# A four-layer graph network on one core: roots on GpSimd, an adjacency scaled once, and another way of ordering the instructions

## The chip, the core and the metric

The kernel runs on one core of a Trainium2 chip. A core has TensorE for matrix products, VectorE and ScalarE for elementwise work, GpSimd (POOL in the profile) and SyncE, whose queue (SP) issues every DMA here. Each engine works through its own list of instructions in order; semaphores tie the lists together. The metric is the device time of one execution in microseconds; the times before are 5736.96, 5727.94 and 5721.77 us, with a median of 5727.94.

## What is computed

Sixty-four graphs of 256 nodes with 128 features, and a symmetric 0/1 adjacency of about 12% ones with a full diagonal, go through four layers. Each layer adds its result to its input and normalizes (`_layernorm`). Cut to what matters:

```python
def layer0(x, adj):      # edge network with a maximum over neighbours
    pre = (x @ (W1 - W2))[:, :, None, :] + (x @ W2)[:, None, :, :] + b
    return max(relu(pre) * adj[..., None], axis=2)

def layer1(x, adj):      # three branches, two of them aggregated
    upd = concat([adj @ elu(x @ W_in.T + b_in), elu(x @ W_node.T + b_node),
                  adj.T @ elu(x @ W_out.T + b_out)])
    return tanh(upd @ W_upd.T + b_upd)

def layer2(x, adj):      # graph convolution with a normalized adjacency
    A = adj + eye;  deg = A.sum(-1)
    dinv = where(deg > 0, rsqrt(deg), 0)
    nA = dinv[:, None] * A * dinv[None, :]
    h = elu(elu(x @ W0 + b0))
    h = elu(nA @ (h @ W1) + b1)
    return nA @ (h @ W2) + b2

def layer3(x, adj):      # a message for every edge, normalized, through gelu
    pre = (x @ W1a)[:, None, :, :] + (x @ W1b)[:, :, None, :] + b1
    msg = gelu(layernorm(pre) * g1 + be1)
    agg = einsum('bijo,bij->bio', msg, adj)
    return layernorm(concat([x, agg]) @ W2 + b2) * g2 + be2
```

## The kernel before

It uses the sparsity. `first` sorts the nodes of a graph by degree (L551 to L560: signs, their sum, a permutation `perm`), ranks every neighbour and writes one-hot columns `hot` (L629): one column of 4800 for every kept slot of every half of the nodes. A product with `hot` then gathers neighbours' values, so layers 0 and 3 work on 2 x 4800 columns and not on 256 x 256 edges.

A graph passes through four stages, each a Python generator: `first` (layer 0: the sort, `hot`, the gathers L665 and the folds of the maximum at L492), `second` (layer 1), `third` (layer 2, the values for layer 3, and the first four tiles of it), `last` (the other tiles and the output). Layer 3's 9600 columns are cut into ten tiles a graph, in each half four of 1024 and one of 704 (`TODO`). For a tile, `sums_of` gathers with L728, adds `dT` at L732 (VectorE), squares (L736, ScalarE), sums over features on TensorE (L743), and makes the variance row at L745 (ScalarE). The row goes to memory (`line<-row`, L750). Two tiles make a pair: the pair's variances come back spread over partitions (`vr<-line`, L762), get a root and a reciprocal (`inverse_root`), are multiplied by the mask `fu` (L769), go out again (`scale_line<-vr`, L771), and each tile's scales return broadcast to all partitions (`rs_s<-scale_line`, L828). In `last`, L839 multiplies a tile by its scales, L841 applies Gelu, and the folds at L492 and the products at L860 gather the messages.

`together` runs the four stages of four successive graphs side by side and so records the instructions of all 64 graphs in one program without a loop. That recorded order isn't the one that runs: when the kernel is built, a scheduler with a model of the engines reorders the instructions of each engine and hands out tile buffers. The order on an engine is then fixed. An ACT_TABLE_LOAD stands before an activation whose function isn't in the table set then loaded; Gelu, the exponential with the hyperbolic tangent, and the root are in three sets.

`inverse_root` is used for layernorms (five a graph, L176), for the degrees (L272) and for pairs of tiles (L768):

```python
def inverse_root(t):
    nc.scalar.activation(t, t, AF.Sqrt)
    nc.vector.reciprocal(t, t)
```

In layer 2 the rows of `hs` are scaled by `dinv` ahead of each of the two products with the adjacency (L293), and the result is scaled once more at L309. The degrees `dg` are summed in `first` (L544); the rest of their work stands in layer 2, two stages later. The adjacency `aT` is used by layer 1 (L238) before layer 2 adds the identity to it (L277).

A second path, `general`, stands behind a test at the end, for inputs that the sparse path doesn't cover; with these inputs it doesn't run. The change touches it where it shares functions.

Of the kernel before, what the change touches and what calls it, by code (L numbers as in the profile page):

```python
# [9 lines left out]
F32 = mybir.dt.float32  # L10
BF16 = mybir.dt.bfloat16
AF = mybir.ActivationFunctionType
ALU = mybir.AluOpType
# [6 lines left out]
P = 128  # L20
EPS = 1e-5
# [22 lines left out]
def kernel(  # L44
# [9 lines left out]
    nc = tc.nc  # L54
    B, N, D = x.shape
    assert N == 2 * P and D == P
    H = N // P
    Q = P // 4

    consts = ctx.enter_context(tc.tile_pool(name="consts", bufs=1))  # L60
# [6 lines left out]
    eps_t = consts.tile([P, 1], F32, name="eps_t")  # L67
    nc.vector.memset(eps_t, EPS)
    minus1 = consts.tile([P, 1], F32, name="minus1")
    nc.vector.memset(minus1, -1.0)  # L70

    def inverse_root(t):

        nc.scalar.activation(t, t, AF.Sqrt)  # L74
        nc.vector.reciprocal(t, t)

    def load(src, shape, name):
        t = consts.tile(shape, F32, name=name)
# [43 lines left out]
    with tc.tile_pool(name="prep", bufs=1) as prep, tc.tile_pool(  # L122
        name="ps_prep", bufs=2, space=bass.MemoryType.PSUM
# [33 lines left out]
    class Shared:  # L157
# [8 lines left out]
        def layernorm(self, dst, src, g=None, be=None):  # L166

            st = self.work.tile([P, H, 6], F32, name="st", bufs=4)
            mv = self.work.tile([P, H, 2], F32, name="mv", bufs=4)
            for h in range(H):  # L170
                nc.vector.bn_stats(st[:, h], src[:, h])
                nc.vector.bn_aggr(mv[:, h], st[:, h])
            rs = self.work.tile([P, H], F32, name="rs", bufs=4)
            nc.vector.tensor_scalar(rs, mv[:, :, 1], EPS, None, ALU.add)
            yield
            inverse_root(rs)  # L176
            yield
            for h in range(H):
                if g is None:
                    nc.vector.tensor_scalar(  # L180
                        dst[:, h], src[:, h], mv[:, h, 0:1], rs[:, h:h + 1], ALU.subtract, ALU.mult
                    )
                else:
                    nc.vector.scalar_tensor_tensor(dst[:, h], src[:, h], mv[:, h, 0:1], g, ALU.subtract, ALU.mult)
                    nc.vector.scalar_tensor_tensor(dst[:, h], dst[:, h], rs[:, h:h + 1], be, ALU.mult, ALU.add)
# [17 lines left out]
        def to_features(self, xn, name, bufs=None):  # L203

            pt = self.psum()
            for h in range(H):
                nc.tensor.transpose(pt[:, h * P:(h + 1) * P], xn[:, h], ident)
            t = self.state.tile([P, N], F32, name=name, **({"bufs": bufs} if bufs else {}))
            nc.scalar.copy(t, pt[:, :N])
            return t  # L210

        def node_tile(self, name):
            return self.state.tile([P, H, P], F32, name=name)
# [44 lines left out]
            yield from self.layernorm(x2, y)  # L258
            s["x2"] = x2

        def layer_2(self, s, aT, deg_of):

            work, psum, elu = self.work, self.psum, self.elu
            x2 = s["x2"]
            deg = work.tile([P, H], F32, name="deg")
            deg_of(deg)
            nc.vector.tensor_scalar(deg, deg, 1.0, None, ALU.add)
            pos = work.tile([P, H], F32, name="pos")
            nc.vector.tensor_scalar(pos, deg, 0.0, None, ALU.is_gt)
            dinv = work.tile([P, H], F32, name="dinv")  # L270
            nc.vector.tensor_scalar(dinv, deg, 1e-30, None, ALU.max)
            inverse_root(dinv)  # L272
            yield
            nc.vector.tensor_mul(dinv, dinv, pos)
            for h in range(H):
                blk = aT[:, h, h * P:(h + 1) * P]
                nc.vector.tensor_add(blk, blk, ident)  # L277
            yield
            xT = self.to_features(x2, "xT_2", 1)
            yield  # L280
            ph = psum()
            hs = work.tile([P, H, P], F32, name="hs")
            for h in range(H):
                cols = slice(h * P, (h + 1) * P)
                nc.tensor.matmul(ph[:, cols], xT[:, cols], w2[0], start=True, stop=True)
            yield
            for h in range(H):
                nc.vector.tensor_add(hs[:, h], ph[:, h * P:(h + 1) * P], b2[0])
            yield from elu(hs, hs, twice=True)
            yield  # L290
            for step in (1, 2):
                for h in range(H):
                    nc.vector.tensor_scalar(hs[:, h], hs[:, h], dinv[:, h:h + 1], None, ALU.mult)  # L293
                pa = psum()
                for h in range(H):
                    nc.tensor.matmul(pa[:, :N], hs[:, h], aT[:, h], start=h == 0, stop=h == H - 1)  # L296
                yield
                agg = work.tile([P, N], F32, name="agg")
                nc.scalar.copy(agg, pa[:, :N])
                yield  # L300
                po = psum()
                for h in range(H):
                    cols = slice(h * P, (h + 1) * P)
                    nc.tensor.matmul(po[:, cols], agg[:, cols], w2[step], start=True, stop=True)
                yield
                hs = work.tile([P, H, P], F32, name="hs")
                for h in range(H):
                    nc.vector.scalar_tensor_tensor(
                        hs[:, h], po[:, h * P:(h + 1) * P], dinv[:, h:h + 1], b2[step], ALU.mult, ALU.add  # L309
                    )  # L310
                if step == 1:
                    yield from elu(hs, hs)
                yield
            nc.vector.tensor_add(hs, hs, x2)
            x3 = self.node_tile("x3")
            yield from self.layernorm(x3, hs)
            s["x3"] = x3
# [36 lines left out]
    def sparse(ctx):  # L354
# [35 lines left out]
        with tc.tile_pool(name="cs_prep", bufs=1) as pp:  # L390
            t = pp.tile([P, P], F32, name="upto_f")
# [4 lines left out]
            t = pp.tile([P, N], I32, name="iota_i")  # L396
# [28 lines left out]
            t = pp.tile([P, 1], F32, name="gbe")  # L425
# [76 lines left out]
        def first(g, s):  # L502
# [37 lines left out]
            nc.scalar.activation(diff, diff, AF.Abs, accum_out=fl[:, 0:1])  # L540
            kc = work.tile([P, H, H], F32, name="kc")
            nc.vector.scalar_tensor_tensor(kc, pc, -1.0, down_c, ALU.mult, ALU.subtract)
            dg = state.tile([P, H], F32, name="dg", bufs=3)
            nc.vector.tensor_reduce(dg, pc, AX.X, ALU.add)  # L544
            s["dg"] = dg

            more = work.tile([P, H, H], F32, name="more")
            for h in range(H):
# [169 lines left out]
        def sums_of(s, i):  # L718
# [47 lines left out]
                s["fulls"].rearrange("h w -> (h w)")[first_at:first_at + n].rearrange("(p k) -> p k", k=PIECE),  # L766
            )
            inverse_root(vr[:rows])  # L768
            nc.vector.tensor_mul(vr[:rows], vr[:rows], fu[:rows])  # L769
            out_line = dram.tile([1, GROUP * TILE], F32, name="scale_line")  # L770
            nc.sync.dma_start(out_line[:, :n].rearrange("o (p k) -> (o p) k", k=PIECE), vr[:rows])  # L771
            at = 0
# [8 lines left out]

        def third(g, s):

            dg = s["dg"]

            def deg_of(deg):
                nc.vector.tensor_scalar(deg, dg, 1.0 / N, None, ALU.mult)

            yield from sh.layer_2(s, s["aT"], deg_of)
            yield  # L790
            x3, perm = s["x3"], s["perm"]

            x3T = sh.to_features(x3, "x3T")
            yield
            pc = psum()
            for h in range(H):
                nc.tensor.matmul(
                    pc[:, h * N:(h + 1) * N], x3T[:, h * P:(h + 1) * P], w3c.rearrange("p c o -> p (c o)"),
                    start=True, stop=True,
                )  # L800
            pcv = pc.rearrange("p (h c o) -> p h c o", h=H, c=2)
            dn = work.tile([P, H, P], F32, name="dn")
            nc.scalar.copy(dn, pcv[:, :, 1])
            c3 = state.tile([P, 3, H, P], BF16, name="c3")
            split3(c3, pcv[:, :, 0])
            yield
            pd = psum()
            for h in range(H):
                for hi in range(H):
                    nc.tensor.matmul(  # L810
                        pd[:, h * N:(h + 1) * N], dn[:, hi], perm[:, h, hi], start=hi == 0, stop=hi == H - 1
                    )
            yield
            dT = state.tile([P, H, N], F32, name="dT")
            nc.scalar.activation(dT, pd.rearrange("p (h n) -> p h n", h=H), AF.Identity, bias=b3c)
            s.update(x3T=x3T, c3=c3, dT=dT)
            yield
            for i in range(AHEAD):
                yield from sums_of(s, i)
# [61 lines left out]
        def steps(g0):  # L881
            ss = [{} for _ in range(U)]
            for u in range(1 - len(STAGES), U):
                together(*[
                    (n, part(g0 + u + i, ss[u + i])) for i, (part, n) in enumerate(STAGES) if 0 <= u + i < U
                ])

        if U == B:
            steps(0)
        else:  # L890
            with tc.For_i(0, B, U) as g0:
                steps(g0)


    def general(ctx):
# [82 lines left out]
        def middle(g, s):  # L978
# [7 lines left out]
                nc.scalar.copy(aT[:, hj], pt[:, :N])  # L986
            yield

            def deg_of(deg):
                nc.vector.tensor_reduce(deg, an, AX.X, ALU.add)  # L990

            yield from sh.layer_1(s, an, aT, s["x1"])
            yield
            yield from sh.layer_2(s, aT, deg_of)
            yield

            x3T = sh.to_features(s["x3"], "x3T")
# [145 lines left out]
```

## Time and profile before

| | |
|---|---|
| median of the three runs | 5727.94 us |
| the profiled execution | 5731.62 us, span 5729.7 us |
| granted TensorE clock, mean | 0.862 |
| DMA | 20% of 16 engines' time, 64 GB/s on average |
| Gelu, L841, 640 tiles | 594.2 us for the 512 into `pre`, 1172 ns each |
| first gathers, L665 | 1052.3 us in 3840 matmuls |
| gathers for layer 3, L728 | 928.8 us in 3840 matmuls |
| adds of dT, L732 | 846.3 us in 1664 instructions |
| scaling by rs_s, L839 | 732.9 us in 640 instructions |
| one-hot columns, L629 | 440.5 us in 1536 instructions |

The profile is of one execution. Its rows of busy time give for each engine the time in which some instruction of it ran; matmuls are pipelined, so a busy TensorE isn't TensorE at its peak. A row of a group reads: line, engine, operation, tile written and tile read, shape, count, then busy time and mean nanoseconds of one, then the time that the engine stood idle ahead of it and what ended the wait. "Waits" list who waited for whom, with the total, the number of times and the longest. The chain is the work that ended last, followed back from the last instruction.

### The profile page before, as it was taken

How to read it: one execution, taken by the hardware profiler on the slowest of the kernel's cores; microseconds unless marked ns; L12 is line 12 of the kernel's file. 1: busy time of each engine (PE TensorE's matmuls, PEld its weight loads, DVE VectorE, ACT ScalarE, POOL GpSimd, SP SyncE). 2: the span in 40 equal slices, each digit the busy share in tenths (PEclk: the TensorE clock that was granted, in tenths of full speed). 3: DMA queues.
4: the chain of work that ended last, by engine and by line, in shares of the span. 5: the costliest groups of instructions: out<-in, count | busy, mean ns of one | idle time of the engine just before them, and what ended most of it. 6: DMA issues, size and time to landing. Idle time of an engine off the chain costs nothing.

```text
span 5729.7 us, 83531 instructions
## 1 busy us (share of the span) xinstructions
PE 4529.9 (79%) x27408; PEld 2508.7 (44%) x27408; DVE 4834.4 (84%) x14654; ACT 4275.2 (75%) x6485; POOL 1.9 (0%) x10
## 2 busy tenths in 40 slices
PE   5878878878778778788788788787887887877875
PEld 2444444444444444444444444444444444444443
DVE  6788888888888888888888888888888888888876
ACT  2577777777777777777777777777777777777785
POOL 0000000000000000000000000000000000000000
PEclk8888889889889889888898898898888887888986
DMA  0122222222212221221221222122212212221222
GB/s 22 44 70 63 62 63 72 62 63 66 69 57 70 65 63 63 72 63 62 63 72 62 63 65 70 59 68 65 63 62 72 64 62 63 69 66 60 68 65 74
DMA packets 292813, 365.15 MB, mean 64 GB/s; under 512 B 151952, under 2 KB 210448, under 8 KB 292368
## 3 DMA queue, kind: packets, MB, share of 16 engines
q1 hardware_dynamic: 292368, 359.73, 20.0%
q8 instruction: 217, 3.56, 0.3%
q14 instruction: 228, 1.87, 0.1%
HBM read 345.07 MB, written 14.53 MB: 63 GB/s over the span
## 4 chain that ended last, share of the span: by engine, by line
PE 52%; DVE 29%; ACT 11%; issue 4%; DMA 3%; SPq 0%; DVEq 0%; POOL 0%; ACTq 0%
PE bigp L665 11%; PE bigp L728 8%; DVE pre L839 6%; PE mm L860 5%; DVE lanes L492 4%; PE mm L743 4%; DVE hot L629 4%; DVE pre L732 4%; DVE sums L492 3%; PE bigp L681 3%; DMA rs_s<-scale_line 2%; PE mm L870 2%; PE mm L296 2%; PE mm L699 2%; PE mm L647 2%
## 5 line engine op out<-in xcount | busy, mean ns | idle before, releaser
L665 PE MATMUL bigp<-hot,q 128*128 128x512 fp8e4 (+1 forms) x3840 | 1052.3, 371 | 66.6 <-DVE lanes L492 52.6
L728 PE MATMUL bigp<-hot,c 128*128 128x512 fp8e4 (+1 forms) x3840 | 928.8, 372 | 140.2 <-DVE pre L732 140.2
L732 DVE TENSOR_TENSOR pre<-bigp,dT 128x512 f32<-128x512 f32 (+6 forms) x1664 | 846.3, 530 | 37.8 <-PE bigp L728 33.5
L492 DVE TENSOR_TENSOR lanes<-bigp,lanes 128x512 f32<-128x512 f32 (+6 forms) x1536 | 772.7, 503 | 94.6 <-PE bigp L681 86.9
L839 DVE TENSOR_TENSOR pre<-pre,rs_s 128x1024 f32<-128x1024 f32 (+1 forms) x640 | 732.9, 1150 | 48.6 <-DMA rs_s<-scale_line 48.0
L736 ACT ACTIVATE sq<-pre 128x1024 f32<-128x1024 f32 (+1 forms) x640 | 638.5, 998 | 169.9 <-DVE pre L732 163.9
L841 ACT ACT_TABLE_LOAD x535 | 686.4, 1283 | 9.5
L492 DVE TENSOR_TENSOR sums<-pre,sums 128x1024 f32<-128x1024 f32 (+6 forms) x1024 | 628.8, 614 | 41.2 <-ACT pre L841 40.7
L745 ACT ACTIVATE row<-mm,eps_t 128x256 f32<-128x256 f32 (+1 forms) x640 | 289.6, 453 | 476.9 <-PE mm L743 476.7
L841 ACT ACTIVATE pre<-pre,be,g 128x1024 f32<-128x1024 f32 (+1 forms) x512 | 594.2, 1172 | 57.8 <-DVE pre L839 53.0
L743 PE MATMUL mm<-sq,ones 128*32 128x256 f32 (+1 forms) x5120 | 482.9, 440 | 135.2 <-ACT sq L736 135.2
L74 ACT ACT_TABLE_LOAD x445 | 570.9, 1283 | 7.5
L728 PEld LDWEIGHTS <-c 128*128 128x128 bf16 x3840 | 331.2, 98 | 550.5 <-issue 136.1
L665 PEld LDWEIGHTS <-q 128*128 128x128 bf16 x3840 | 310.8, 97 | 392.6 <-issue 112.0
L296 PE MATMUL mm<-aT,hs 128*128 128x256 f32 x512 | 232.3, 600 | 316.1 <-DVE hs L293 214.8
L629 DVE TENSOR_SCALAR hot<-rank 128x512 fp8e4<-128x512 bf16 (+5 forms) x1536 | 440.5, 348 | 0.0
L681 PEld LDWEIGHTS <-pick 42*128 42x128 bf16 x2944 | 155.8, 95 | 481.5 <-issue 474.2
L296 PEld LDWEIGHTS mm<-aT,hs 128*128 128x128 f32 x512 | 135.6, 293 | 425.8 <-issue 316.1
L860 PE MATMUL mm<-w3u,sums 128*128 128x128 f32 x2048 | 296.7, 289 | 18.4 <-DVE sums L492 16.1
L194 ACT ACT_TABLE_LOAD x221 | 283.5, 1283 | 3.9
L681 PE MATMUL bigp<-lack,pick 42*128 42x36 bf16 (+16 forms) x2944 | 285.7, 187 | 0.0
L860 PEld LDWEIGHTS mm<-w3u,sums 128*128 128x128 f32 x2048 | 254.5, 195 | 37.3 <-issue 17.6
(226 smaller groups left out, 7132.6 us busy)
## 6 DMA issues: line engine op xcount, KB each, us to landing
rs_s<-scale_line SPq DMA_DIRECT2D x512, 512.0 KB
rs_s<-scale_line SPq DMA_DIRECT2D x128, 352.0 KB
an<-in_adj SPq DMA_DIRECT2D x64, 256.0 KB
x<-in_x SPq DMA_DIRECT2D x64, 128.0 KB
line<-row SPq DMA_DIRECT2D x512, 4.0 KB
out<-o SPq DMA_DIRECT2D x64, 128.0 KB
fu<-fulls SPq DMA_DIRECT2D x192, 4.0 KB
vr<-line SPq DMA_DIRECT2D x192, 8.0 KB
```

The lines of the kernel that those rows point to most:

```text
L74: nc.scalar.activation(t, t, AF.Sqrt)
L492: nc.vector.tensor_tensor(lanes[:, :k, :w], src[:, i:i + k], lanes[:, :k, :w], op)
L629: nc.vector.tensor_scalar(hot[:, :, at:at + w], rank[:, :, :w], s0 + i + 1.0 - FAR, None, ALU.is_equal, saturate=False)
L665: nc.tensor.matmul(pt[:, :tl], q3[:, i, h], hot[:, h, t0:t0 + tl], start=i == 0, stop=False)
L681: nc.tensor.matmul(o_, l_, r_, start=False, stop=i == len(todo) - 1)
L728: nc.tensor.matmul(pt[:, :bl], c3[:, k, h], hot[:, h, t0 + b:t0 + b + bl], start=k == 0, stop=k == 2)
L732: nc.vector.tensor_add(block(pre[:, b:], n, w, at), block(pt, n, w, at), widen(dT[:, h, :w], n))
L736: nc.scalar.activation(sq[:, :tl], pre[:, :tl], AF.Square)
L743: nc.tensor.matmul(pr[q * Q:(q + 1) * Q, :tl // 4], ones[:, :Q], v4[:, :, q], start=True, stop=True)
L839: nc.vector.tensor_mul(pre[:, :tl], pre[:, :tl], rs[:, :tl])
L841: nc.scalar.activation(msg[:, :tl], pre[:, :tl], AF.Gelu, bias=be3, scale=g3)
L860: nc.tensor.matmul(pt[:, cols], lanes[:, k, cols], w3u[:, 1], start=k == 0, stop=False)
```

## The change

Five edits:

- `inverse_root` becomes one power of -0.5 on GpSimd, against a constant tile. It now serves the pairs and the degrees alone. The multiplication of a pair's scales by the mask goes to GpSimd as well.
- A layernorm takes its root on ScalarE with the small constant as the activation's bias, which drops an addition on VectorE; the reciprocal stays there. Where the generator yields also changes.
- The degrees' inverse root moves from layer 2 to `first`, into `inverse_root_of`, and its product with the mask goes to GpSimd. The result lives in four buffers until layer 2 takes it.
- In layer 2, `dinv` is multiplied into the rows of the adjacency once, in two instructions of 128x256, in place of scaling `hs` ahead of both products in four of 128x128.
- The unrolled body stands in a block of its own, for which the scheduler orders instructions with a finer model of the engines.

```diff
+    mhalf = consts.tile([P, 16], F32, name="mhalf")
+    nc.vector.memset(mhalf, -0.5)
+
     def inverse_root(t):
 
-        nc.scalar.activation(t, t, AF.Sqrt)
-        nc.vector.reciprocal(t, t)
+        nc.gpsimd.tensor_tensor(t, t, mhalf[:t.shape[0], :t.free_size()], ALU.pow)
...
                 nc.vector.bn_stats(st[:, h], src[:, h])
                 nc.vector.bn_aggr(mv[:, h], st[:, h])
+            yield
             rs = self.work.tile([P, H], F32, name="rs", bufs=4)
-            nc.vector.tensor_scalar(rs, mv[:, :, 1], EPS, None, ALU.add)
-            yield
-            inverse_root(rs)
-            yield
+            nc.scalar.activation(rs, mv[:, :, 1], AF.Sqrt, bias=eps_t)
+            yield
+            nc.vector.reciprocal(rs, rs)
...
+        def inverse_root_of(self, deg, bufs):
+
+            nc.vector.tensor_scalar(deg, deg, 1.0, None, ALU.add)
+            pos = self.work.tile([P, H], F32, name="pos")
+            nc.vector.tensor_scalar(pos, deg, 0.0, None, ALU.is_gt)
+            dinv = self.state.tile([P, H], F32, name="dinv", bufs=bufs)
+            nc.vector.tensor_scalar(dinv, deg, 1e-30, None, ALU.max)
+            inverse_root(dinv)
+            nc.gpsimd.tensor_mul(dinv, dinv, pos)
+            return dinv
...
-        def layer_2(self, s, aT, deg_of):
+        def layer_2(self, s, aT, dinv_of):
...
-            deg = work.tile([P, H], F32, name="deg")
-            deg_of(deg)
-            nc.vector.tensor_scalar(deg, deg, 1.0, None, ALU.add)
-            pos = work.tile([P, H], F32, name="pos")
-            nc.vector.tensor_scalar(pos, deg, 0.0, None, ALU.is_gt)
-            dinv = work.tile([P, H], F32, name="dinv")
-            nc.vector.tensor_scalar(dinv, deg, 1e-30, None, ALU.max)
-            inverse_root(dinv)
-            yield
-            nc.vector.tensor_mul(dinv, dinv, pos)
+            dinv = dinv_of()
+            yield
             for h in range(H):
                 blk = aT[:, h, h * P:(h + 1) * P]
                 nc.vector.tensor_add(blk, blk, ident)
+            for h in range(H):
+                nc.vector.tensor_scalar(aT[:, h], aT[:, h], dinv[:, h:h + 1], None, ALU.mult)
...
             for step in (1, 2):
-                for h in range(H):
-                    nc.vector.tensor_scalar(hs[:, h], hs[:, h], dinv[:, h:h + 1], None, ALU.mult)
                 pa = psum()
...
-            dg = state.tile([P, H], F32, name="dg", bufs=3)
+            dg = work.tile([P, H], F32, name="dg")
             nc.vector.tensor_reduce(dg, pc, AX.X, ALU.add)
-            s["dg"] = dg
+            nc.vector.tensor_scalar(dg, dg, 1.0 / N, None, ALU.mult)
+            s["dinv"] = sh.inverse_root_of(dg, 4)
...
             inverse_root(vr[:rows])
-            nc.vector.tensor_mul(vr[:rows], vr[:rows], fu[:rows])
+            nc.gpsimd.tensor_mul(vr[:rows], vr[:rows], fu[:rows])
...
-            dg = s["dg"]
-
-            def deg_of(deg):
-                nc.vector.tensor_scalar(deg, dg, 1.0 / N, None, ALU.mult)
-
-            yield from sh.layer_2(s, s["aT"], deg_of)
+            yield from sh.layer_2(s, s["aT"], lambda: s["dinv"])
...
         if U == B:
-            steps(0)
+            with tc.block(name="graphs", schedule_with_timeline_sim=True):
+                steps(0)
```

More of the change, by code (lines that the diff above doesn't have):

```diff
@@ L987, in middle, with dinv_of @@
             yield
-            def deg_of(deg):
+            def dinv_of():
+                deg = work.tile([P, H], F32, name="deg")
                 nc.vector.tensor_reduce(deg, an, AX.X, ALU.add)
+                return sh.inverse_root_of(deg, 1)
             yield from sh.layer_1(s, an, aT, s["x1"])
             yield
-            yield from sh.layer_2(s, aT, deg_of)
+            yield from sh.layer_2(s, aT, dinv_of)
             yield
```

## The prediction

> **What bounds the kernel now.** I read the busy rows and the chain first, then the groups with their table loads, then who waited for whom on VectorE, then one pair of tiles in order of time.
>
> ```profile
> PE 4529.9 (79%) x27408; PEld 2508.7 (44%) x27408; DVE 4834.4 (84%) x14654; ACT 4275.2 (75%) x6485; POOL 1.9 (0%) x10
> ...
> PE 52%; DVE 29%; ACT 11%; issue 4%; DMA 3%; SPq 0%; DVEq 0%; POOL 0%; ACTq 0%
> ...
> L841 ACT ACT_TABLE_LOAD x535 | 686.4, 1283 | 9.5
> L74 ACT ACT_TABLE_LOAD x445 | 570.9, 1283 | 7.5
> L194 ACT ACT_TABLE_LOAD x221 | 283.5, 1283 | 3.9
> ```
>
> No engine is full: VectorE is nearest, TensorE close behind, ScalarE has 1236 table loads (the three rows and 35 smaller ones), 1586 us of its 4275. The chain jumps among all three, so the end is set by VectorE's work plus what it waits at hand-offs.
>
> One graph takes 87.35 us: in the chain, the same sixteen L728 matmuls begin at 2812.28 and, two graphs on, at 2986.94. 64 x 87.35 = 5590, which leaves 140 us of the 5730 for filling and emptying. In the steady part VectorE works 775.20 of 900 us, 75.2 us a graph, and idles 12.1:
>
> ```profile
> 1900.00:2800.00 900.00, 725.39 (x4464) 401.47 (x4462) 775.20 (x2335) 694.27 (x1048) 0.00 (x0) 0.89 0.21 66
> ```
>
> VectorE's waits (total us, times, longest):
>
> ```profile
> DVE io L226 <- PE mm L223: 179.7, 64, 3.1
> DVE rest L498 <- ACT q L497: 93.4, 54, 3.4
> DVE lanes L492 <- PE bigp L681: 86.9, 172, 2.0
> DVE y L330 <- PE mm L870: 72.1, 64, 4.9
> DVE fl L604 <- PE mm L599: 51.0, 64, 2.7
> DVE elu_e L200 <- ACT elu_e L194: 50.2, 42, 1.5
> DVE pre L839 <- DMA rs_s<-scale_line: 48.0, 57, 4.2
> ```
>
> Over the view, 506 us are waits for TensorE, 283 for ScalarE, 52 for DMAs. Several happen once a graph at the same place: the instruction stood too early in VectorE's order for what feeds it.
>
> **What the Trainium skill says.** "ScalarE: Activation LUTs", What ACT_TABLE_LOAD costs, gives about 1283 ns for a load; the trace agrees (1283). Its further 1380 ns drain per switch is no row here, and I charge nothing for it. "SBUF — State Buffer", Who interferes with whom: a VectorE instruction with two SBUF inputs, or in a two-port mode, and a GpSimd instruction that reads SBUF exclude each other for the whole instruction. No row here shows it, as POOL does nothing. "GPSIMD Engine Reference", section 3.1, has 4497 ns for a two-input add of 2048 elements; I found no price for a power.
>
> **The change, part by part, per graph unless said.**
>
> *ScalarE.* The built program holds 516 table loads (253 Gelu, 195 root, 66 exponential, 2 others) against 1236: the new order puts functions of one set together and five pair roots and a degree root leave. 720 x 1.283 = 924 us. The roots themselves are 320 of some 0.21 us and 64 of about 0.20: 81 us. ScalarE falls from 4275 to 3270 us. The bias added to the layernorm root costs nothing that I can see. As ScalarE isn't the bound, this pays only in waits for it. VectorE's waits for ScalarE without L498's (counted below) are 283 - 93 = 190 us, 3.0 a graph; L75's wait for the pair root (25) must go, and I let half go in all: **-1.5** (0 to -3.0).
>
> *VectorE.* Removed:
>
> ```profile
> L75 DVE RECIPROCAL vr<-vr 128x16 f32<-128x16 f32 (+1 forms) x320 | 78.4, 245 | 29.5 <-ACT vr L74 25.4
> L293 DVE TENSOR_SCALAR hs<-hs,dinv 128x128 f32<-128x128 f32 x256 | 61.0, 270 | 2.2
> L769 DVE TENSOR_TENSOR vr<-vr,fu 128x16 f32<-128x16 f32 (+1 forms) x320 | 52.9, 165 | 0.3
> L174 DVE TENSOR_SCALAR rs<-mv 128x2 f32<-128x2 f32 x320 | 51.1, 160 | 0.1
> L75 DVE RECIPROCAL dinv<-dinv 128x2 f32<-128x2 f32 x64 | 9.4, 146 | 2.0 <-ACT dinv L74 2.0
> ```
>
> With the degree multiply L274 (6.4) that is 259 us in 1344 instructions. Added: the adjacency scaling, 128 of 128x256, which like L560 (72.7 us in 256, same shape, a per-partition scalar) cost 0.284 each: 36 us. Net 223. But neighbours overlap on this engine: the groups' busy times sum to 5654 against the row's 4834, 56 ns for each of 14654. 1216 fewer instructions give back 68. So 155 us, **-2.4**. The four small degree operations only move, into the first stage.
>
> *The order.* I added up VectorE's group times (less 56 ns each) between what starts a hand-off's chain and the instruction that waits, in both built programs. From the first layernorm's output to io: 2.9 us before, 4.8 after; the wait was 179.7/64 = 2.8, so 1.9 go. From the exponential's hs (L293 before, L201 after) to rest of q: 1.0 to 3.4; that wait, 1.46, goes. From the last sums to y L330: 4.2 to 6.2; the wait, 1.1, goes. From perm to fl: 1.5 to 1.2; 0.3 more. Together **-4.0** (0 if the engine merely waits at the next instruction, as before).
>
> *TensorE.* Same 20,685 matmuls. But between its adds for tiles 0 and 7 VectorE now has some 26 us of work and TensorE 32 (before 34 and 31); from tile 7 to 8 it is 29 against 16.5 (before 23.5 and 17). The first stretch is now set by TensorE, 6 us over. Four PSUM buffers of three 0.386 us matmuls let it run ahead by 4.6, so 1.4 to 6 remain, partly waits counted above: **+1.7**.
>
> *GpSimd.* Twelve small instructions: five powers and five multiplies of 16 columns, one of each of 2. For 16 columns the page's slope adds 35 ns, so the fixed part and the power decide. Bounds: 0.2 us, as on VectorE, and 3 us for the power; I take 1.0, and 0.3 for a multiply, 7.4 us in all. Two-input SBUF rows (L839 733, L492 sums 629) and SBUF-to-SBUF scalar rows (L629 441, L560, L180, L200, L201 and the scaling, some 480) make 47% of VectorE's time; at 86% busy, at most 7.4 x 0.47 x 0.86 = 3.0 us of blocking. POOL also loses some of these races: **+2.0** (0.5 to 7.1, the last with 3 us powers).
>
> *The scales' way round.* A pair of tiles sends its variances through HBM and back. One pair before, in order of time (its last add ends at 2814.48):
>
> ```profile
> 2814.58 1.06 ACT L736 ACTIVATE sq<-pre 128x1024 f32<-128x1024 f32 x1 [1.26 <-DVE pre L732]
> ...
> 2818.58 0.53 SPq L750 DMA_DIRECT2D line<-row  x1
> ...
> 2820.29 0.32 SPq L762 DMA_DIRECT2D vr<-line  x1
> ...
> 2823.30 0.20 ACT L74 ACTIVATE vr<-vr 128x16 f32<-128x16 f32 x1
> ...
> 2824.84 0.33 SPq L771 DMA_DIRECT2D scale_line<-vr  x1
> ...
> 2826.25 0.32 SPq L828 DMA_DIRECT2D rs_s<-scale_line  x1
> ```
>
> Square 1.2, sums and row 2.9 here (1.9 where ScalarE is prompt), line to vr 1.7, landing 3.0, roots 1.5, store 1.4, and 3.9 for the last load (issued 2829.76, VectorE released 2833.62): 14.6 to 15.6 us. After, with POOL at 1.3 in place of 1.5, 14.4 at best. Between a pair's last add and its first L839 the new order leaves VectorE 9.8 to 11.8 us of work at the tightest pair (tiles 8 and 9), where the old left 15 to 18; but TensorE has 13 to 14.3 us there, which sets that stretch anyway: **+0.4** (0 to 2 and more as POOL slows). On SP's queue the store of the scales waits for POOL, and row stores and scale loads queue behind it, as they did behind L769.
>
> *Sum.* -1.5 - 2.4 - 4.0 + 1.7 + 2.0 + 0.4 = -3.8, so 83.55 us a graph: 64 x 83.55 + 140 = 5487 us of span against 5730. The profiled execution took 5731.6, the median of three is 5727.9, so about 5485 of median. A change is told from none at about 0.3%, 17 us.
>
> **Rivals.**
> *More than that, 5160 us:* ScalarE's table loads held up the whole hand-over. All its 3.0 us go, TensorE's stretch hides, POOL costs 0.5: -3.0 - 2.4 - 4.0 + 0.5 = -8.9, 78.45 us a graph. For it: 14 us a graph of ScalarE freed, and TensorE too waits 248 us for ScalarE. Against: TensorE's waits are mostly for VectorE (923 us). Chance 0.15.
> *No gain, 5740 us:* the hand-off waits move to the next instruction, as the same chains feed them; without the -4.0 the sum is +0.2. For it: the new order bunches VectorE's work in one stretch, TensorE's in another. Against: four measured waits have other work put in front. Chance 0.15.
> *Slower, 5940 us:* the power on GpSimd takes 3 us. It keeps the shared port, so VectorE loses up to 7.1 us a graph, 5.1 more than reckoned, and the tight pair's scales come 2 us later: -3.8 + 5.1 + 2.0 = +3.3, 90.65 us a graph. Each further microsecond of a power costs about 3.0 (five blocks at 0.40 each, and the pair), so this decides from 2.3 us. For it: nothing in the trace prices it, and VectorE's largest rows need that port. Against: sixteen columns only. Chance 0.17.
> That the change doesn't act is out: loads and instructions are counted in the built program.
>
> **How the numbers follow.** The forecast has 0.53. Its own range is 5330 to 5660, from the bounds above. The slow case and the lower half of the fast one make up what may be left out, so 5200 to 5830. Faster: 0.15, most of 0.53 (0.51), and 0.06 of the case without gain, 0.72. Same: 0.05. Slower: 0.17 and 0.06 of that case, 0.23.
>
> **What would show it.** ScalarE near 3270 us with 516 loads; VectorE's row near 4680 us, more if blocking lengthens L839 and sums (1.22 us each before); POOL's power rows near 1 us; io, q and y waiting under 60 us each; L839's wait for its DMA staying under 100 us. The forecast is wrong if powers take over 2 us, if L839's waits grow by hundreds, or if the four waits stand elsewhere with the same sum.

## The result: slower by an eighth

The changed kernel takes 6445.36 us (median of four runs, 6437.86 to 6449.48), the kernel before 5725.73 beside it: a ratio of 1.1252, interval 1.1231 to 1.1272. The forecast was 5485, with a range of 5200 to 5830. The profiled execution of the changed kernel has a span of 6436.1 us against 5729.7, 706 more, at a mean granted TensorE clock of 0.810 against 0.862.

The busy rows and the chain of the changed kernel, from its page:

```profile
PE 4754.8 (74%) x27408; PEld 2624.8 (41%) x27408; DVE 4788.0 (74%) x13439; ACT 3340.8 (52%) x5381; POOL 1289.7 (20%) x778
...
issue 35%; DMA 20%; POOL 16%; DVE 14%; PE 12%; ACT 2%; SPq 1%; POOLq 0%; DVEq 0%; ACTq 0%
```

Before, TensorE and VectorE stood at 79% and 84% and made up 81% of the chain. Now both are at 74%, ScalarE has lost 934 us of work, and the chain runs through POOL and DMAs: the kernel waits more, and for latencies. In the steady part (one stretch of 900 us, busy time of PE, PEld, DVE, ACT and POOL, then the clock, the DMA share and GB/s) VectorE works 672 us where it worked 775, TensorE 667 where it worked 725:

```profile
1900.00:2800.00 900.00, 667.38 (x3879) 367.85 (x3879) 671.97 (x1888) 474.44 (x768) 182.36 (x108) 0.81 0.19 57
```

VectorE's waits in the changed kernel (total us, times, longest). A line's number has moved by one to six: L840 is the former L839, L738 L732, L239 L226, L503 L498, L335 L330, L610 L604.

```profile
DVE pre L840 <- DMA rs_s<-scale_line: 961.3, 436, 7.4
DVE pre L738 <- PE bigp L734: 158.1, 131, 2.6
DVE elu_e L202 <- ACT elu_e L196: 90.3, 127, 1.3
DVE rs L179 <- ACT rs L177: 74.5, 135, 1.7
...
DVE y L335 <- PE mm L871: 7.9, 1, 7.9
DVE fl L610 <- PE mm L605: 4.6, 4, 1.6
DVE io L239 <- PE mm L236: 4.2, 5, 1.3
DVE rest L503 <- ACT q L502: 2.9, 1, 2.9
```

The waits for io, rest and y were to fall, and did; fl's, which was to grow by 0.3 us a graph, went as well. Together they fell from 396 to 20 us. But one wait that was 48 us is 961. Summed over the whole view, VectorE's waits went from 842 to 1581 us: for DMAs from 52 to 965, for ScalarE from 283 to 316, for TensorE from 506 to 298. These 739 us more, less 46 of busy time, are the 706 within 13 us.

One of the waits in order of time, the chain of a pair of tiles on all engines (start, duration, engine, line, what, in brackets the idle time before it and its releaser). VectorE's last add of the pair ends at 3148.7:

```profile
3148.81 1.06 ACT L742 ACTIVATE sq<-pre 128x1024 f32<-128x1024 f32 x1 [1.51 <-DVE rs L179]
...
3151.22 0.47 ACT L751 ACTIVATE row<-mm,eps_t 128x256 f32<-128x256 f32 x1 [1.35 <-PE mm L749]
...
3153.40 0.32 SPq L768 DMA_DIRECT2D vr<-line  x1
...
3156.35 2.90 POOL L77 TENSOR_TENSOR vr<-vr,mhalf 128x16 f32<-128x16 f32 x1 [19.83 <-DMA vr<-line]
...
3159.32 0.22 POOL L775 TENSOR_TENSOR vr<-vr,fu 128x16 f32<-128x16 f32 x1
...
3159.57 0.33 SPq L777 DMA_DIRECT2D scale_line<-vr  x1
...
3161.03 0.32 SPq L829 DMA_DIRECT2D rs_s<-scale_line  x1
...
3165.05 1.23 DVE L840 TENSOR_TENSOR pre<-pre,rs_s 128x1024 f32<-128x1024 f32 x1 [3.32 <-DMA rs_s<-scale_line]
```

Every link goes as soon as the one before allows: row to line 1.7 us, landing 3.0 (here long; 1.7 in the median at this pair), power 2.9, product 0.2, store 1.5, load 4.0. From the last add to L840 it is 16.3 us here. This is a graph's first pair (tiles 0 and 1); over the 54 graphs in the middle of the run it takes 15.2 us in the median (14.4 to 17.0), the last pair (tiles 8 and 9) 15.0 (13.7 to 16.5), and VectorE has 10.7 and 10.3 us of other work meanwhile. But the wait isn't that of these two pairs alone. Summed for each of a graph's five pairs, in the order of the tiles, L840 waits 172, 262, 311, 73 and 143 us; before it was 1, 11, 26, 5 and 5.

### The profile page after: what moved, and what is told of

Its sections match the earlier page's. It is cut to its first block, busy times and chain, and to the rows that moved or that the text cites. A ratio compares the mean times of both kernels' runs of the same rounds, so it can differ in the third digit from the quotient of the medians.

```text
span 6436.1 us, 82199 instructions
## 1 busy us (share of the span) xinstructions
PE 4754.8 (74%) x27408; PEld 2624.8 (41%) x27408; DVE 4788.0 (74%) x13439; ACT 3340.8 (52%) x5381; POOL 1289.7 (20%) x778
## 4 chain that ended last, share of the span: by engine, by line
issue 35%; DMA 20%; POOL 16%; DVE 14%; PE 12%; ACT 2%; SPq 1%; POOLq 0%; DVEq 0%; ACTq 0%
POOL vr L77 14%; DMA rs_s<-scale_line 13%; PE bigp L671 5%; DVE pre L840 4%; DMA scale_line<-vr 3%; DVE sums L497 2%; PE bigp L734 2%; DMA line<-row 2%; DVE pre L738 2%; DMA vr<-line 2%; DVE lanes L497 2%; POOL vr L775 1%; PE bigp L687 1%; PE mm L749 1%; POOL dinv L77 1%
## 5 line engine op out<-in xcount | busy, mean ns | idle before, releaser
L77 POOL TENSOR_TENSOR vr<-vr,mhalf 128x16 f32<-128x16 f32 (+1 forms) x320 | 1121.6, 3505 | 4284.4 <-DMA vr<-line 4272.9
L840 DVE TENSOR_TENSOR pre<-pre,rs_s 128x1024 f32<-128x1024 f32 (+1 forms) x640 | 740.6, 1157 | 965.8 <-DMA rs_s<-scale_line 961.3
L671 PE MATMUL bigp<-hot,q 128*128 128x512 fp8e4 (+1 forms) x3840 | 1116.3, 399 | 389.1 <-ACT q L502 218.7
L734 PE MATMUL bigp<-hot,c 128*128 128x512 fp8e4 (+1 forms) x3840 | 965.6, 390 | 16.2 <-DVE pre L738 15.5
L738 DVE TENSOR_TENSOR pre<-bigp,dT 128x512 f32<-128x512 f32 (+6 forms) x1664 | 831.8, 533 | 158.7 <-PE bigp L734 158.1
L671 PEld LDWEIGHTS <-q 128*128 128x128 bf16 x3840 | 353.5, 103 | 788.9 <-ACT q L502 234.9
L209 PE MATMUL mm<-ident,x 128*128 128x128 f32 x512 | 156.7, 405 | 545.4 <-DVE x L182 531.2
L734 PEld LDWEIGHTS <-c 128*128 128x128 bf16 x3840 | 349.9, 102 | 458.2 <-issue 188.1
L749 PE MATMUL mm<-sq,ones 128*32 128x256 f32 (+1 forms) x5120 | 461.9, 439 | 42.4 <-ACT sq L742 42.0
L301 PE MATMUL mm<-aT,hs 128*128 128x256 f32 x512 | 255.5, 653 | 276.4 <-DVE hs L203 276.4
L209 PEld LDWEIGHTS mm<-ident,x 128*128 128x128 f32 x512 | 78.9, 195 | 623.1 <-issue 548.8
```

Of the source, the lines that this page charges most:

```text
L77: nc.gpsimd.tensor_tensor(t, t, mhalf[:t.shape[0], :t.free_size()], ALU.pow)
L671: nc.tensor.matmul(pt[:, :tl], q3[:, i, h], hot[:, h, t0:t0 + tl], start=i == 0, stop=False)
L734: nc.tensor.matmul(pt[:, :bl], c3[:, k, h], hot[:, h, t0 + b:t0 + b + bl], start=k == 0, stop=k == 2)
L738: nc.vector.tensor_add(block(pre[:, b:], n, w, at), block(pt, n, w, at), widen(dT[:, h, :w], n))
L749: nc.tensor.matmul(pr[q * Q:(q + 1) * Q, :tl // 4], ones[:, :Q], v4[:, :, q], start=True, stop=True)
L840: nc.vector.tensor_mul(pre[:, :tl], pre[:, :tl], rs[:, :tl])
```

## The experiments

Three theories stood at the start. A: the power on GpSimd is the loss (it lengthens the scales' way round). B: the new order of the instructions is the loss by itself. C: GpSimd's use of the shared port lengthens VectorE's instructions. Later came D: what the new order loses is the lead that it gives a pair ahead of L840. All ratios are to the kernel before, on the same chip.

### The same order, the power made cheap

```diff
+    for fn in nc.m.functions:
+        for b in fn.blocks:
+            row = b.instructions
+            for n, i in enumerate(row):
+                if i.opcode == "TensorTensor" and i.op == ALU.pow and "vr" in str(i.outs[0]):
+                    row[n] = type(i)(op=ALU.mult, **{k: getattr(i, k) for k in FIELDS})
+            b.instructions = row
```

`FIELDS` names the fields that a copied instruction keeps. The degrees' powers stay powers.

> The changed kernel's instructions in exactly its order, but each pair's power on GpSimd (320 of 3.5 us) is a product by the same tile: the pair's root is left out of the scales, the way round is 3.2 us shorter, nothing else differs. Theory A (the power lengthens the pair's way round past the work that this order leaves VectorE): the waits of L840 for rs_s fall from 961 us to under 350 and the time to 5450 to 5850 us. Theory B (the new order itself bunches the work, whatever the power takes): L840's waits go but others come, and the time stays above 6150. Theory C (GpSimd keeps VectorE off the shared port): the mean of L840 and of the sums at L497 falls below 1157 and 618 ns; VectorE's busy time falls by 100 us or more.

It took 5923.24 us, ratio 1.0348 (1.0331 to 1.0366). POOL's rows for `vr`, from what reads and writes that tile (ns min/median/max), in the changed kernel and then in this one:

```profile
L77 POOL TENSOR_TENSOR vr<-vr,mhalf x320: 2898/3399/4925, 194.1 to 6400.9; 128x16 f32<-128x16 f32 x96, 108x16 f32<-108x16 f32 x64
```

```profile
L77 POOL TENSOR_TENSOR vr<-vr,mhalf x320: 220/223/2117, 194.5 to 5893.4; 128x16 f32<-128x16 f32 x96, 108x16 f32<-108x16 f32 x64
```

A power of sixteen columns takes 2.9 us at least and 3.4 in the median, a product of the same operands 0.22. So in this order the power costs 522 us, 1.6 us for each of 320, about half of its length. L840 still waits 376 us and the kernel is still 200 us slower than before: A is a large part and not the whole, and both figures lie just outside what A expected. At the first and the last pair the wait falls from 315 us to 52, at the second and third from 573 only to 311: there the order itself is late. As this kernel leaves out the root, other values flow through what follows, and its granted clock is 0.843 against 0.810; how much of the 522 us is the clock's wasn't tried.

C falls with the page's groups. Here is the scaling by rs_s in the kernel before, in the changed one and in this one:

```profile
L839 DVE TENSOR_TENSOR pre<-pre,rs_s 128x1024 f32<-128x1024 f32 (+1 forms) x640 | 732.9, 1150 | 48.6 <-DMA rs_s<-scale_line 48.0
```

```profile
L840 DVE TENSOR_TENSOR pre<-pre,rs_s 128x1024 f32<-128x1024 f32 (+1 forms) x640 | 740.6, 1157 | 965.8 <-DMA rs_s<-scale_line 961.3
```

```profile
L840 DVE TENSOR_TENSOR pre<-pre,rs_s 128x1024 f32<-128x1024 f32 (+1 forms) x640 | 737.4, 1153 | 379.6 <-DMA rs_s<-scale_line 375.7
```

The longest single one takes 1240 ns in the changed kernel and took 1227 before, so none was held up for the length of a power.

### The order alone, and the edits without it

```diff
         if U == B:
-            steps(0)
+            with tc.block(name="graphs", schedule_with_timeline_sim=True):
+                steps(0)
```

This line is the whole change to the kernel before in the first of these runs, and it is the only part of the change left out in the second.

> The kernel before with only the block ordered by the finer model; roots stay on ScalarE and VectorE, and nothing of the computation differs. 824 table loads in place of 1236. Theory A: the order is good where the way round has no power in it: 5350 to 5700 us. Theory B: the order is what loses: above 6000 us, with VectorE waiting at L839 for rs_s.

> All edits of the change but the block with the finer model: power on GpSimd, adjacency scaled once, order by the former model; 767 table loads. Theory A: the former order leaves 15 to 18 us of VectorE's work ahead of a pair's use, so a power of 3.5 us is covered but for some waits: 5500 to 5850 us, L840 waiting 100 to 500 us. Theory B: faster than before, 5400 to 5650 us. Theory C: VectorE's rows longer, 5800 us or more.

The order alone took 6317.17 us, 1.104 (1.1021 to 1.1058); all edits in the former order 5816.74, 1.0166 (1.0149 to 1.0183). Beside 5724 the order adds 593 and the edits 93; together they add 721. B holds for the order: no power runs on GpSimd in the first, and it loses most of what the change loses. In the second, B had expected a gain; there A's expectation holds, with 284 us of waits at L840. With the order alone VectorE waits where it does in the changed kernel, and for the root on ScalarE too:

```profile
DVE pre L839 <- DMA rs_s<-scale_line: 475.2, 238, 5.3
DVE vr L75 <- ACT vr L74: 268.0, 179, 4.8
DVE sums L492 <- ACT pre L841: 174.4, 126, 2.3
```

### The pairs' root put back

```diff
-            inverse_root(vr[:rows])
-            nc.gpsimd.tensor_mul(vr[:rows], vr[:rows], fu[:rows])
+            nc.scalar.activation(vr[:rows], vr[:rows], AF.Sqrt)
+            nc.vector.reciprocal(vr[:rows], vr[:rows])
+            nc.vector.tensor_mul(vr[:rows], vr[:rows], fu[:rows])
```

Once in the changed kernel, with the finer model's order, and later once with the former order.

> The changed kernel with the finer model, but the pairs' roots back as square root on ScalarE and reciprocal and product on VectorE; degrees stay on GpSimd; 754 table loads. Theory A: without the power the finer order gains: 5300 to 5650 us, L840 waiting under 350 us. Theory B: above 6000 us.

> All edits except two: the former model of order, and the pairs' roots left on ScalarE and VectorE (the degrees' roots and their masks stay on GpSimd, the layernorms' bias and the adjacency scaled once stay). If what lost was the finer order and the pairs' power, and the other edits are a gain of about 78 us (5895 with the pairs' power alone, 5817 with all edits, both in the former order), this comes to 5640 to 5670 us, a ratio near 0.987, with VectorE's row some 100 to 130 us shorter than before and no wait for the scales over 100 us. The rival says that the other edits' gain exists only beside a kernel that already waits for the scales, and that alone they do nothing: 5710 to 5740.

With the finer order 6282.63 us, 1.0978 (1.096 to 1.0996): the order made for a root on ScalarE loses about as much as the order alone. With the former order 5718.87, 0.9988 (0.9979 to 0.9997): the rival of that run was right. The other edits take 68 us from VectorE's row (4766.5 against 4834.4) and 172 from ScalarE's, and VectorE's waits grow by 69 (842 to 911 over the view; the largest rise is y's, from 72 to 173, while io's fall from 180 to 111). The saved work came back as waiting at hand-offs.

### The pairs' power alone, in the former order

```diff
-            inverse_root(vr[:rows])
-            nc.vector.tensor_mul(vr[:rows], vr[:rows], fu[:rows])
+            nc.gpsimd.tensor_tensor(vr[:rows], vr[:rows], mhalf[:rows, :PIECE], ALU.pow)
+            nc.gpsimd.tensor_mul(vr[:rows], vr[:rows], fu[:rows])
```

> The kernel before, with only the pairs' root as a power on GpSimd and the mask's product there, in the former order (766 table loads). Theory D: the leads of 15 to 17 us just cover a way round with a power of some 3.1 us, so the saved table loads are about given back: 5650 to 5850 us. If the layernorms' and the adjacency's edits were what lost 93 us in the former order: 5600 to 5720 us.

5894.74 us, 1.0302 (1.0272 to 1.0331), above both expected ranges. VectorE's first wait there, 48 us before:

```profile
DVE pre L842 <- DMA rs_s<-scale_line: 585.8, 144, 7.2
```

Of this, 565 us stand at tiles 2 to 5, the pairs that were the closest to waiting before (37 of the 48 us). So a root of 2.9 us in a place where the former order had a chain just short enough costs 169 us net of the table loads saved, though GpSimd had nothing else to do. Its cost is latency, not throughput.

### Longer leads

Theory D was tried by letting the order be made as if each pair had one, two or four powers more on its way, and running only these added ones as products with ones (mostly 0.22 to 0.27 us each). The pair's own power stays a power (3.0 to 3.1 us in the median), so the leads grow and the chain hardly does. The edit for two:

```diff
+    once = consts.tile([P, 16], F32, name="once")
+    nc.vector.memset(once, 1.0)
...
             inverse_root(vr[:rows])
+            nc.gpsimd.tensor_tensor(vr[:rows], vr[:rows], once[:rows], ALU.pow)
+            nc.gpsimd.tensor_tensor(vr[:rows], vr[:rows], once[:rows], ALU.pow)
```

> The changed kernel ordered by the finer model as if one more power of a pair's scales followed the first; in the program itself that second one is a product by a tile of ones, so what is computed is the same and POOL works some 0.4 to 0.7 us longer a pair. In the built order VectorE has 13.2 and 13.7 us of work ahead of the first use of the first and of the last pair, against 10.9 and 10.5 in the changed kernel (17.3 and 17.4 before). Theory D (the finer order leaves too little work ahead of a pair's use, so VectorE waits for the pair's way round): L840's waits for rs_s fall from 961 us to 600 to 800 and the time to 6100 to 6300 us. Theory B (the bunching of the work loses, not the lead): within 80 us of 6445.

> The same with two more powers reckoned when ordering, both products by ones when run. The leads are 16.3 and 17.8 us, about those of the kernel before. Theory D: L840's waits fall to 150 to 450 us, the time to 5600 to 5850 us. Theory B: above 6250 us.

> The same with four more powers reckoned and four products by ones run. The leads are 20.3 and 28.9 us. Theory D: L840's waits fall under 100 us, and what the change saves on ScalarE and VectorE shows: 5350 to 5650 us. Theory B: above 6250 us.

They took 6374.74 (1.1135, 1.1108 to 1.1162), 6535.14 (1.1404, 1.1366 to 1.1442) and 6731.06 us (1.1754, 1.1725 to 1.1783). As the pair's own power runs in them, they are to be held against the changed kernel's 6445. In the built orders VectorE's work ahead of the tightest pair did grow, from some 11 us to 13 with one, 16 with two and 20 with four, and the wait for the scales fell from 961 us to 317, 252 and 294. But the time fell by 71 us with one and rose by 90 and 286 with two and four, outside all of D's ranges and inside B's. D falls as the account of the loss: VectorE's waits for TensorE rose from 298 us to 676, 1030 and 784 instead. As each of the three is an order of its own, they don't price a lead by itself. With two more, VectorE's waits and then TensorE's:

```profile
DVE y L338 <- PE mm L876: 338.9, 64, 8.5
DVE pre L845 <- DMA rs_s<-scale_line: 251.9, 186, 9.8
```

```profile
PE mm L304 <- DVE hs L206: 657.9, 127, 11.8
PE mm L212 <- DVE x L185: 558.7, 65, 11.0
```

TensorE waits for a layernorm's output (x) and an exponential's (hs), VectorE for layer 3's last products (y).

### A cheap root in the former order, and a finer order made for it

The first run puts the same products into the exact order of all edits with the former model (the edit of the first experiment, on the kernel without the finer model). The second writes the product in the source, so that the finer model knows that there is no power:

```diff
-            inverse_root(vr[:rows])
+            nc.gpsimd.tensor_tensor(vr[:rows], vr[:rows], mhalf[:rows, :PIECE], ALU.mult)
```

> The exact instruction order of all edits with the former model of order, with the 320 powers of the pairs turned into products of the same operands, so that the root of the scales is left out. It prices the power in the former order. If the power's cost there is what the former order loses by it (5895 - 5724 = 171 us), this comes to about 5650 us; the finer order, at 5923 with the same products, then still loses some 270 us, under half of what it loses with the scales' chain as it was: the order's loss and the chain's length then add to each other. If the finer order's loss is its own and has nothing to do with the chain, this comes to about 5330 us (5923 - 593), which would make the former order with a cheap root much faster than before.

> All edits, with the pairs' power written as a product (the root of the scales is left out), so that the finer order is made for the product and not for the power. Differs from the product put into the order made for the power (5923 us) only in the order. If the loss lies in the finer order as such, 5850 to 6000 us, and the same waits as there (scales 376 us). If the order made for the power was bad because the model priced that power wrongly, the one made for the product is well below: under 5750.

The former order took 5633.51 us, 0.9841 (0.9823 to 0.986), with 42.5 us of waits for the scales, close to the 5650 expected if the power costs there what it costs alone. The finer order made for the product took 6586.31, 1.1494 (1.1467 to 1.1522), 663 us more than the order made for the power with the same work in it but for 190 table loads more (706 against 516). Neither expectation held: not the same loss with the same waits, and not a better order. So a wrong price for the power doesn't explain the loss; given the true operation the finer model made a worse order. What misleads it isn't shown. Its TensorE:

```profile
PE mm L209 <- DVE x L182: 889.1, 92, 16.0
PE mm L301 <- DVE hs L203: 403.3, 66, 7.6
```

### What the finer orders have in common

| kernel | us | TensorE waits for x, hs | VectorE waits for scales |
|---|---|---|---|
| former order, cheap root | 5634 | 115, 155 | 43 |
| former order, pairs' root back | 5719 | 95, 190 | 14 |
| kernel before | 5724 | 108, 215 | 48 |
| former order, all edits | 5817 | 112, 159 | 284 |
| former order, pairs' power alone | 5895 | 99, 186 | 586 |
| finer, made for the power, cheap root | 5923 | 440, 279 | 376 |
| finer, pairs' root back | 6283 | 491, 290 | 525 |
| finer, order alone | 6317 | 542, 317 | 475 |
| finer, one more reckoned, power kept | 6375 | 449, 480 | 317 |
| changed kernel | 6445 | 531, 276 | 961 |
| finer, two more, power kept | 6535 | 559, 658 | 252 |
| finer, made for the product | 6586 | 889, 403 | 691 |
| finer, four more, power kept | 6731 | 504, 637 | 294 |

The wait for x stands at one place of every graph, where layer 0 ends: the products L705 (L699 before) give the maxima, VectorE and ScalarE normalize, and the transposes L209 (L207) of the result follow. TensorE's own list there, in the kernel before:

```profile
2815.49 1.95 PE L699 MATMUL mm<-mk,permT 128*128 128x128 f32 x16
2817.37 0.64 PE L743 MATMUL mm<-sq,ones 128*32 128x256 f32 x8
2817.94 1.90 PE L728 MATMUL bigp<-hot,c 128*128 128x512 fp8e4 x8
2820.56 0.82 PE L728 MATMUL bigp<-hot,c 128*128 128x512 fp8e4 x3 [0.72 <-DVE pre L732]
2822.52 0.81 PE L728 MATMUL bigp<-hot,c 128*128 128x512 fp8e4 x3 [1.14 <-DVE pre L732]
2824.78 0.33 PE L207 MATMUL mm<-ident,x 128*128 128x128 f32 x1 [1.45 <-DVE x L180]
```

and in the changed kernel:

```profile
3067.33 1.05 PE L705 MATMUL mm<-mk,permT 128*128 128x128 f32 x8
3068.22 0.38 PE L734 MATMUL bigp<-hot,c 128*128 128x512 fp8e4 x1
3078.15 0.45 PE L209 MATMUL mm<-ident,x 128*128 128x128 f32 x1 [9.55 <-DVE x L182]
```

The former order keeps 22 matmuls of another graph's tiles for these seven us, 4.2 us of work; the changed kernel has put them in front, has one left and stands for 9.55 us. Counted over all graphs, 21 or 22 matmuls lie in that gap in the median in all five kernels with the former order; in the eight with the finer one the average is at most 14, and in four of them the median is 0 or 1. This is seen in the traces; moving those matmuls back alone wasn't tried, so how much of the order's loss this one place makes isn't shown.

## Why the prediction was wrong

*The order, "Together -4.0" a graph: this step failed first.* Three of its waits fell as it said, io by more, and fl, which it had growing, went too: 376 us in all, 5.9 a graph (the step's own terms add up to 4.2). But four hand-offs are not the order. It was priced by what stands in front of the waits that the old order had, not by the waits that the new one makes. Alone it costs 593 us, 9.3 a graph. Its rival, "the hand-off waits move to the next instruction", named the kind of thing and not the size.

*The scales' way round, "+0.4": failed as well.* L840's wait rose by 913 us, 14.3 a graph, where under 100 us in all was forecast. At the pair that the step takes up, tiles 8 and 9, its sums were nearly right. The chain is 15.0 us in the median against 14.4 at best, in part by luck: GpSimd's share is 3.1 us and not 1.3, but `vr<-line` lands in 1.6 and not in 3.0. The work ahead is 10.3 us against 9.8 to 11.8, and TensorE is busy for 14.7 of the 15.0 us against 13 to 14.3. That pair waits 143 us, 2.2 a graph. The step took it for the only one in danger. The other four pairs wait 819 us, most of it at tiles 2 to 5. There VectorE has more work ahead, at least 15.5 and 24.3 us, but the pair's last row is made at least 11 and 22 us after its last add, where it takes 3 at tiles 8 and 9. The kernel before gave a sign of it: of its 48 us of this wait, 37 stood at these two pairs and 5 at tiles 8 and 9.

*GpSimd, "I take 1.0": the size was off, the path too.* A power takes 2.9 us at least and 3.4 in the median, and 179 of the 320 pass the upper bound of 3. The slower rival had that length and a point of 2.3 us from which it decides, and its 2 us for the later scales came as 2.2 at tiles 8 and 9. But the larger part of its loss, 5.1 us a graph of VectorE blocked at the shared port, did not show: L840 at 1157 ns against 1150, the sums at 618 against 614. With 5940 us against 6445 it had the direction in part by luck. The power's price is in the chain. It is 183 us in the former order (5817 less 5634), where almost only tiles 2 and 3 wait for it (256 us with the power, 30 without), and 522 in the finer one, where each of the five pairs waits 60 to 156 us more with it. So the two losses add to more than singly.

So the 721 us (6445 less 5724) divide, along one path through the runs, into -90 for the edits with the root left out in the former order, +290 for the finer order and +522 for the power in it. By another path the shares differ; 339 of the last figure are there only because the order is that one.

*ScalarE, "-1.5": the counts right, the gain absent.* 516 loads as forecast, 3341 us against 3270. VectorE's waits for ScalarE without those for q rose from 190 to 313 us.

*VectorE, "-2.4": a term mis-sized.* The groups sum to 5383 us (forecast 5431), but the row is 4788 and not 4680: neighbours overlap by 44 ns an instruction and not by 56. The order alone shows the same, 5596 less 4954.5 over 14654, which is 44, while the former order with all edits keeps 53. In the eight kernels with the finer order it is 40 to 46 ns, in the five with the former one 52 to 58: the engine's row goes with the order.

*TensorE, "+1.7":* VectorE's waits for TensorE fell by 208 us, though L738's, in the stretch meant, rose from 34 to 158. The step's idea that TensorE gets the longer part is right in that place and small beside the rest. Its "20,685 matmuls" stand in no trace; both have 27408, so that they are the same holds.

Of the kernels that compute the whole result only one comes in below the kernel before, the former order with the pairs' root put back, and by a tenth of a per cent.

## What to carry to other kernels

A change of order is priced by the whole list of hand-offs, new ones first: for every chain with a latency, compare it with the work that the new order leaves ahead of its end, for every use in a graph and not for the one with the least work ahead. Here the small waits before the change already showed which chains had no slack left. Work moved to an idle engine is free only where its latency is covered; a slow operation on a chain through memory costs up to its length at every pair whose lead is shorter than the chain. Keep a reordering apart from the edits beside it when measuring, since here one line alone lost six times what the four other edits did without it.

## What the runs showed of the hardware

A power on GpSimd takes 2.90 us at least for 128x16 and 0.70 for the degrees' 128x2, some 157 ns a column by an estimate from the two; a product of 16 columns takes 0.22.

```profile
L77 POOL TENSOR_TENSOR dinv<-dinv,mhalf x64: 695/697/1156, 39.3 to 6149.4; 128x2 f32<-128x2 f32 x64
```

The Trainium skill, "SBUF — State Buffer", Who interferes with whom, says that a VectorE instruction with two inputs in SBUF and a GpSimd instruction that reads SBUF exclude each other. These traces show it in one direction only. In the changed kernel 112 powers begin while a full L840 or sums instruction (128x1024) runs that still has over 0.3 us to go. They take 3.77 us in the median, and nine in ten of them end 2.755 to 2.758 us after that instruction does: GpSimd waits until VectorE has finished. The other way round VectorE doesn't wait. In the former order with all edits 71 such instructions begin inside a power; they take 1.21 to 1.24 us, much as without one, and a power that had not been held up itself stays at 2.90. So a power doesn't keep VectorE out for its whole length, though the slower rival was reckoned so. One case of each, from the changed kernel and from the former order with all edits:

```profile
2022.80 1.22 DVE L840 TENSOR_TENSOR pre<-pre,rs_s 128x1024 f32<-128x1024 f32 x1 [0.41 <-DMA rs_s<-scale_line]
2023.01 3.77 POOL L77 TENSOR_TENSOR vr<-vr,mhalf 128x16 f32<-128x16 f32 x1 [8.56 <-DMA vr<-line]
```

```profile
2023.11 2.90 POOL L77 TENSOR_TENSOR vr<-vr,mhalf 108x16 f32<-108x16 f32 x1 [11.36 <-DMA vr<-line]
2024.18 1.22 DVE L840 TENSOR_TENSOR pre<-pre,rs_s 128x1024 f32<-128x1024 f32 x1
```

The granted clock is lower in the slower kernels: 0.86 at a span of 5632 to 5730 us, 0.84 at 5809 to 5925, 0.81 to 0.83 from 6281 up. TensorE's row grew from 4530 to 4755 us, by 5.0%, with the same 27408 matmuls, while the granted clock fell by 6.0%, from 0.862 to 0.810. No run tells which is cause here, or how much of the loss goes with the clock.
